# Turning a normalized input by blocks on VectorE instead of on TensorE, in a graph-network layer on one core

## The chip, the cores and the metric

The kernel runs on one core of one Trainium2 chip. The metric is the device time of the whole program in microseconds (us), taken as the median of three runs: 2178.12 us before the change (2177.3 to 2178.31). The profile of the kernel before is of one execution with a span of 2177.0 us.

A core has five engines that run side by side, each through its own list of instructions in a fixed order: TensorE (PE in the profile; its weight loads are listed as PEld), VectorE (DVE), ScalarE (ACT), GpSimd (POOL) and SyncE (SP). Transfers between the on-chip memory (SBUF) and the device memory (DRAM) run on 16 DMA engines; SP, ACT and POOL issue them.

## The reference

For each of 32 graphs ("batches", `b`), with 512 nodes of 256 features:

```python
h = maximum(layernorm(x), 0)            # x: (32, 512, 256), normalized over the features
hc = transpose(h)                       # features first
c  = relu(bn1(conv1d(hc, conv1_w)))     # 1 tap
c  = bn2(conv1d(c, conv2_w, pad 8))     # 17 taps along the nodes
x_conv = transpose(relu(c + hc))
s  = h @ w_se.T + b_se                  # 3 features
A  = exp(-dist(s, s)) * adj             # 512 x 512 for each graph
x_nmp = A @ relu(h @ w_msg.T + b_msg)
out = x + GRU(input=[x_conv, x_nmp], state=h)   # three gates of 256
```

Everything is in float32. What the change touches is the first two lines: each graph's input is normalized with nodes on the partitions (a partition is one of the 128 rows of SBUF), and everything after it wants `h` with the features on the partitions.

## The kernel before

The program lays out its own order of instructions: Python generators ("streams") for the rows, the begins, the graphs, the convolution and the gates take turns, and a clock called `now`, which counts what TensorE's instructions should take, decides which comes next. `yield t` means "go on with other streams until `now` has reached t". The order that results is fixed when the program is built.

The beginning of a graph, from its transfer to the turned and stored copy:

```python
def fetch(b, xs=None):
    XS[b] = front.tile([P, NT, D], F32, name="x_sb", bufs=2) if xs is None else xs
    nc.sync.dma_start(XS[b], x[b].rearrange("(c p) d -> p c d", p=P))

def load(b, xs=None):
    if b not in XS:
        fetch(b, xs)
    NORMS[b] = norm(b)
    NORM_AT[b] = now + 7.0 if b >= G else ARRIVES[b]      # G = 4

def norm(b):
    ...     # VectorE: statistics and rstd; GpSimd: the power of -1/2
    for c in range(NT):                                   # NT = 4
        act.activation(xs[:, c, :], xs[:, c, :], AF.Identity, bias=shift[:, c : c + 1],
                       scale=rstd[:, c : c + 1])
    ...

def norm_t(b, d):
    xn = XS[b]
    if d == 0:
        HT[b] = front.tile([P, ND, N], F32, name="hT", bufs=2)
    ps = bank()                                           # a PSUM bank, "ps_g", 3 of them
    for c in range(NT):
        turn(ps[:, c * P : (c + 1) * P], xn[:, c, d * P : (d + 1) * P])   # TensorE
    act.activation(HT[b][:, d, :], ps, AF.Relu)           # ScalarE
    if d == ND - 1:                                       # ND = 2
        XS.pop(b)
        nc.gpsimd.dma_start(HD[b], HT[b])                 # to DRAM, read again later

def begin(b):
    ...
    yield lambda: b not in NORMS
    yield NORM_AT[b]
    for d in range(ND):
        norm_t(b, d)
        ...         # after the last: begun = b + 1, load(b + 4) or load(b + 2)
        yield now
```

The turned copy in DRAM, `HD[b]`, is read three times: by the first convolution (`load_row`, four graphs at a time), by the messages (`load_graph`) and by the gates (`load_gates`).

Two pieces of the kernel already work by blocks of 32 by 32: from graph 8 on (`TURNED = 8`) the adjacency is loaded in such blocks and turned by VectorE, and so are the output and the residual. A block load, and the last stores:

```python
def blocks(t, dram_b, o, store):
    for g in range(P // 32):
        at = o * P + 32 * g
        a = t[32 * g : 32 * g + 32, :].rearrange("i (k j) -> i k j", j=32)
        d = dram_b[:, :, at : at + 32]
        nc.sync.dma_start(*((d, a) if store else (a, d)))

def store(y, o, s):
    for g in range(P // 32):
        at = slice(32 * g, 32 * g + 32)
        nc.gpsimd.dma_start(OB[b][:, s.start // 32 : s.stop // 32, o * P + 32 * g : ...],
                            y[at, s].rearrange("i (k j) -> i k j", j=32))
```

The graph's stream waits for the first four graphs, because their inputs 2 and 3 lie in its tile `at`:

```python
# graph(b)
    factors_t()
    if b < 1:
        yield lambda: begun >= G
    yield act.free + LAG
    at = front.tile([P, NT, N], F32, name="at", bufs=1)
    kernel_exp(at)                    # four small matmuls, then ScalarE's exp
...
# start of the program
    spare = front.tile([P, NT, N], F32, name="at", bufs=1).rearrange("p c (k d) -> p (c k) d", d=D)
    for b in (2, 3):
        load(b, spare[:, (b - 2) * NT : (b - 1) * NT, :])
```

In the last graph's last gate the products come in two halves, and both halves go to one PSUM tile:

```python
    ps_n = acc.tile([P, N], F32, name="ps_acc")
    ...
    for h in range(2):
        s = slice(h * N // 2, (h + 1) * N // 2)
        for j in range(2 * ND):
            matmul(ps_n[:, s], wih[:, j, cols(o, 2)], x_in[j][:, s], ...)
        mix(s)                        # VectorE reads ps_n[:, s]; then tanh, mixing, store
```

Of the kernel before, what the change touches and what calls it, by code (L numbers as in the profile page):

```python
# [8 lines left out]
F32 = mybir.dt.float32  # L9
AF = mybir.ActivationFunctionType  # L10
# [3 lines left out]
P = 128  # L14
# [17 lines left out]
G = 4  # L32
# [3 lines left out]
TURNED = 8  # L36
# [8 lines left out]
def kernel(  # L45
# [28 lines left out]
    nc = tc.nc  # L74
    B, N, D = x.shape
    NT = N // P
    ND = D // P
# [4 lines left out]
    NZ = 2 * NH  # L82
# [3 lines left out]
    front = ctx.enter_context(tc.tile_pool(name="front", bufs=2))  # L86
    cv = ctx.enter_context(tc.tile_pool(name="cv", bufs=1))
    dram = ctx.enter_context(tc.tile_pool(name="dram", bufs=1, space=bass.MemoryType.DRAM))
    cps = ctx.enter_context(tc.tile_pool(name="cps", bufs=2, space=PSUM))
    bps = ctx.enter_context(tc.tile_pool(name="bps", bufs=1, space=PSUM))  # L90
    acc = ctx.enter_context(tc.tile_pool(name="acc", bufs=2, space=PSUM))
# [6 lines left out]
    now = 5.0  # L98
# [23 lines left out]
    dve, act = Engine(nc.vector, 0.12, 0.00108), Engine(nc.scalar, 0.16, 0.0009)  # L122
# [30 lines left out]
    XS, HT, HB, HR, HG, XN, XR = {}, {}, {}, {}, {}, {}, {}  # L153
    NORMS, NORM_AT = {}, {}
    ARRIVES = (0.0, 7.0, 11.0, 13.0)
    HD = {b: dram.tile([P, ND, N], F32, name=f"hd{b}") for b in range(B)}
    ND_ = {(b, d): dram.tile([P, N], F32, name=f"nd{b}_{d}") for b in range(B) for d in range(ND)}
    begun = told = 0

# [4 lines left out]
    def load(b, xs=None):  # L164
        if b not in XS:
            fetch(b, xs)
        NORMS[b] = norm(b)
        NORM_AT[b] = now + 7.0 if b >= G else ARRIVES[b]

    def load_row(b):  # L170
        HR[b] = front.tile([P, ND, N], F32, name="hT", bufs=2)
        nc.sync.dma_start(HR[b], HD[b])

# [99 lines left out]
    def norm(b):  # L273

        xs = XS[b]
        st = front.tile([P, NT, 6], F32, name="st")
        mv = front.tile([P, NT, 2], F32, name="mv")
        for c in range(NT):
            dve.bn_stats(st[:, c, :], xs[:, c, :])
            dve.bn_aggr(mv[:, c, :], st[:, c, :])  # L280
            if c % 2:
                yield 0.0
        rstd = front.tile([P, NT], F32, name="rstd")
        rsqrt(rstd, mv[:, :, 1])
        yield dve.free + 2.0
        shift = front.tile([P, NT], F32, name="shift")
        dve.scalar_tensor_tensor(
            shift, mv[:, :, 0], -1.0, rstd, op0=ALU.mult, op1=ALU.mult
        )
        yield dve.free + 0.2  # L290
        for c in range(NT):
            act.activation(
                xs[:, c, :], xs[:, c, :], AF.Identity, bias=shift[:, c : c + 1],
                scale=rstd[:, c : c + 1],
            )
            if c % 2:
                yield act.free + LAG
# [291 lines left out]
    xs = all_operands()  # L589
# [174 lines left out]
    XB = x.rearrange("b (k i) d -> b i k d", i=32)  # L764
    OB = out.rearrange("b (k i) d -> b i k d", i=32)

    def blocks(t, dram_b, o, store):
        for g in range(P // 32):
            at = o * P + 32 * g
            a = t[32 * g : 32 * g + 32, :].rearrange("i (k j) -> i k j", j=32)  # L770
            d = dram_b[:, :, at : at + 32]
            nc.sync.dma_start(*((d, a) if store else (a, d)))

    def load_res(b, o):
        if b < B and (b, o) not in XR:
            XR[b, o] = late.tile([P, N], F32, name="res", bufs=3)
            blocks(XR[b, o], XB[b], o, False)

    def begin(b):

        nonlocal begun
        if b == 2:
            yield lambda: told > 0
        yield lambda: b not in NORMS
        yield NORM_AT[b]
        for d in range(ND):
            norm_t(b, d)
            if d == ND - 1:  # L790
                begun = b + 1

                later_b = b + 4 if b < 2 else b + 2 if b >= G else B
                if later_b < B:
                    load(later_b)
            yield now

    def rows(b):
# [8 lines left out]
    def graph(b):  # L807

        nonlocal told
        yield lambda: begun > b  # L810
        if b == 0:
            HG[0] = HT[0]
            yield act.free + LAG
        elif b not in HG:
            load_graph(b)
            yield now + 9.0
        msg = front.tile([P, NT, D], F32, name="msg", bufs=1)
        for c in range(NT):
            messages(b, msg, c)
            yield now  # L820
        told = b + 1
        factors()
        load_graph(b + 1)
        yield dve.free + LAG
        factors_t()
        if b < 1:
            yield lambda: begun >= G
        yield act.free + LAG
        at = front.tile([P, NT, N], F32, name="at", bufs=1)
        kernel_exp(at)  # L830
        yield act.free + 0.3
        for n in range(NT):
            masked(b, at, n)
            if n < NT - 1:
                yield dve.free - 0.2
        settle()
        yield dve.free + LAG
        for d in range(ND):
            gather(b, msg, at, d)
            yield now  # L840

    def gates(b):
# [4 lines left out]
        hT = HB[b]  # L847
# [51 lines left out]
        def store(y, o, s):  # L899
            for g in range(P // 32):  # L900
                at = slice(32 * g, 32 * g + 32)
                nc.gpsimd.dma_start(  # L902
                    OB[b][:, s.start // 32 : s.stop // 32, o * P + 32 * g : o * P + 32 * g + 32],
                    y[at, s].rearrange("i (k j) -> i k j", j=32),
                )
            if s.stop == N:
                del XR[b, o]
                load_res(b + 1, o)

        for o in range(ND):  # L910
            r = z = None

            def reset():
                nonlocal r
                settle()
                r = late.tile([P, N], F32, name="r", bufs=2)
                act.activation(r, ps_r, AF.Sigmoid, bias=brz[:, o : o + 1])

            def reset_hidden():
                dve.scalar_tensor_tensor(  # L920
                    r, ps_h, vec[:, _COL["b_hh"] + 2 * ND + o : _COL["b_hh"] + 2 * ND + o + 1], r,
                    op0=ALU.add, op1=ALU.mult,
                )

            def update():
                nonlocal z
                z = late.tile([P, N], F32, name="z")
                act.activation(z, ps_z, AF.Sigmoid, bias=brz[:, ND + o : ND + o + 1])

            def mix(s=slice(0, N)):  # L930
                dve.tensor_tensor(r[:, s], ps_n[:, s], r[:, s], op=ALU.add)
                later(dve.free + 0.3, lambda r=r, z=z, o=o: mix_next(r, z, o, s))
                if o == ND - 1:
                    load_sums(b + 1, 0)
                    load_sums(b + 1, 1)

            ps_r = acc.tile([P, N], F32, name="ps_acc")
            if o == 0:
                yield lambda: b in evacuated
                yield evacuated[b]  # L940
                yield from residual()
                yield from products(ps_r, o, 0, 0, 1, (0, 2))
                yield act.free + LAG
            else:
                yield from products(ps_r, o, 0, 0, 1, (0, 2))
            yield from products(ps_r, o, 0, 1, 3, (0, 2), reset)
            ps_h = acc.tile([P, N], F32, name="ps_acc")
            yield from products(ps_h, o, 2, 0, 1, (0, 0), reset_hidden)
            ps_z = acc.tile([P, N], F32, name="ps_acc")
            yield from products(ps_z, o, 1, 0, 3, (0, 2), update)  # L950
            if o == 0:
                load_gates(b + 1)
            ps_n = acc.tile([P, N], F32, name="ps_acc")
            if b < B - 1 or o < ND - 1:
                yield from products(ps_n, o, 2, 1, 3, (1, 2), mix)
                continue

            for h in range(2):
                s = slice(h * N // 2, (h + 1) * N // 2)
                for j in range(2 * ND):  # L960
                    matmul(
                        ps_n[:, s], wih[:, j, cols(o, 2)], x_in[j][:, s],
                        start=(j == 0), stop=(j == 2 * ND - 1),
                    )
                mix(s)
                yield now
            settle()
# [96 lines left out]
    )  # L1064
    NORM_AT[0] = act.free + LAG
    load(1)
    spare = front.tile([P, NT, N], F32, name="at", bufs=1).rearrange("p c (k d) -> p (c k) d", d=D)
    for b in (2, 3):
        load(b, spare[:, (b - 2) * NT : (b - 1) * NT, :])
    nc.sync.dma_start(wmsg[:, :, :D], w_msg)  # L1070
    nc.sync.dma_start(wmsg[:, :, D:], w_se)
    nc.sync.dma_start(bmsg[:, :D], b_msg.to_broadcast([P, D]))
# [6 lines left out]
    while streams:  # L1079
# [7 lines left out]
        name = min(able, key=lambda k: clock[k])  # L1087
# [63 lines left out]
```

## Time and profile before

| engine | busy, us | what it does here |
|---|---|---|
| TensorE (PE) | 2113.7 | all products, and the turns of inputs and of the first 8 adjacencies |
| VectorE (DVE) | 1494.1 | transforms of the convolution, mixing of gates, block turns |
| ScalarE (ACT) | 784.4 | normalization, exp, gates, copies out of PSUM |
| GpSimd (POOL) | 282.9 | small powers, and the issue of stores |

A row of the profile's group list names the program line, the engine, the operation, the tile written and the tiles read, the shape and the count, then busy time and mean duration of one, then how long the engine stood idle just before and what released it. A matmul's listed duration includes its way through a pipeline, so the distance between the starts of two matmuls, read from the timeline, tells what one costs TensorE. Names such as L118, L127 and L132 are those of helpers through which nearly all instructions pass, so that the tile names tell the instructions apart. The timeline lists instructions in order of time: start, length, engine, line, operation, tiles, how many were merged, and in brackets the idle time before the first of them.

### The profile page before, as it was taken

The numbers are of one execution on the slowest core, as the hardware profiler recorded it, in microseconds if no ns is written. First come the engines' busy times: TensorE is split into PE (matmuls) and PEld (weight loads), VectorE is DVE, ScalarE is ACT, GpSimd is POOL, SyncE is SP. The second block draws the span as 40 slices with busy tenths as digits, with TensorE's granted clock in tenths as the row PEclk, the third lists the DMA queues.
The fourth block names the chain that finished last, engine by engine and source line by source line (L and its number), as shares of the span: only waits on it lengthen the run. The fifth ranks groups of instructions, "written<-read, shape, count | busy, mean of one in ns | idle before, by whom it ended". The sixth has DMA issues, their size and how long they took to land.

```text
span 2177.0 us, 26672 instructions
## 1 busy us (share of the span) xinstructions
PE 2113.7 (97%) x9392; PEld 1314.7 (60%) x9392; DVE 1494.1 (69%) x2770; ACT 784.4 (36%) x1323; POOL 282.9 (13%) x429
## 2 busy tenths in 40 slices
PE   6999899999999999999999999999999999999997
PEld 3877666566665666656665666656666566665443
DVE  6696886676766767667875777757777677776333
ACT  6445332433233443234424253243522324223211
POOL 2000111111101111101111111101111010011112
PEclk9999999999999999999999999999999999999999
DMA  6346655556574556655665655655565555554231
GB/s 254 143 152 222 204 181 181 159 144 176 153 205 138 146 156 176 189 159 137 180 167 171 185 157 158 178 140 169 158 172 150 150 160 144 151 154 97 61 71 34
DMA packets 432709, 341.94 MB, mean 157 GB/s; under 512 B 351424, under 2 KB 368192, under 8 KB 431936
## 3 DMA queue, kind: packets, MB, share of 16 engines
q1 hardware_dynamic: 408928, 270.23, 45.0%
q0 software_dynamic: 20048, 56.91, 8.4%
q10 hardware_dynamic: 3600, 13.11, 1.5%
q8 instruction: 74, 1.21, 0.2%
q14 instruction: 59, 0.48, 0.1%
HBM read 270.16 MB, written 69.99 MB: 156 GB/s over the span
## 4 chain that ended last, share of the span: by engine, by line
PE 58%; issue 31%; DVE 4%; POOL 3%; ACT 2%; DMA 2%; ACTq 0%; POOLq 0%; SPq 0%; DVEq 0%
PE ps_acc L127 25%; PE ps_g L127 14%; PE ps_c L127 12%; PE ps_b L127 5%; POOL out_dram L902 3%; PE ps_g L132 2%; DMA x_sb<-in_x_dram 1%; PE ps_b L732 1%; DVE x L118 1%; DVE g L118 1%; POOL nd L760 0%; ACT y L118 0%; DVE gg L118 0%; DVE at L118 0%; DVE z L118 0%
## 5 line engine op out<-in xcount | busy, mean ns | idle before, releaser
L127 PE MATMUL ps_acc<-xconv,wih 128*128 128x512 f32 (+1 forms) x772 | 363.5, 593 | 5.8 <-ACT xconv L118 5.2
L127 PE MATMUL ps_acc<-xnb,wih 128*128 128x512 f32 (+1 forms) x772 | 362.5, 592 | 0.0
L127 PE MATMUL ps_acc<-hTb,whh 128*128 128x512 f32 x768 | 355.7, 593 | 0.8 <-ACT r L118 0.8
L127 PE MATMUL ps_c<-xd,w 128*128 128x116 f32 x2800 | 343.0, 276 | 0.0
L127 PEld LDWEIGHTS ps_c<-xd,w 128*128 128x128 f32 x2800 | 328.6, 193 | 3.0 <-issue 2.2
L902 POOL DMA_DIRECT2D out_dram<-res x260 | 169.0, 656 | 1005.0 <-DVE res L118 889.2
L118 DVE TENSOR_TENSOR r<-ps_acc,r 128x512 f32<-128x512 f32 (+1 forms) x65 | 44.4, 684 | 367.3 <-PE ps_acc L127 367.3
L127 PE MATMUL ps_g<-at,msg 128*128 128x512 f32 x512 | 232.0, 602 | 9.6 <-DVE at L118 7.7
L127 PEld LDWEIGHTS ps_acc<-xconv,wih 128*128 128x128 f32 x772 | 141.7, 191 | 160.7 <-issue 149.4
L127 PEld LDWEIGHTS ps_acc<-xnb,wih 128*128 128x128 f32 x772 | 141.2, 189 | 157.9 <-issue 156.3
L127 PEld LDWEIGHTS ps_acc<-hTb,whh 128*128 128x128 f32 x768 | 141.3, 190 | 147.5 <-issue 142.1
L127 PEld LDWEIGHTS ps_b<-x,w 128*128 128x128 f32 x1400 | 182.8, 192 | 68.9 <-issue 53.4
L118 ACT ACTIVATE mid<-ps_b 128x232 f32<-128x232 f32 x175 | 64.0, 366 | 350.4 <-PE ps_b L127 322.3
L127 PE MATMUL ps_b<-x,w 128*128 128x116 f32 x1400 | 184.1, 275 | 5.1 <-ACT at L118 4.7
L127 PEld LDWEIGHTS ps_g<-at,msg 128*128 128x128 f32 x512 | 97.0, 193 | 125.2 <-issue 111.2
L118 DVE SCALAR_TENSOR_TENSOR x<-x,x 128x480 f32<-128x480 f32 (+1 forms) x184 | 144.2, 784 | 3.0
L118 DVE TENSOR_TENSOR x<-x 128x240 f32<-128x240 f32 (+1 forms) x320 | 134.9, 463 | 0.4
L127 PE MATMUL ps_g<-wmsg,hTg 128*128 128x259 f32 x496 | 124.3, 382 | 0.0
L127 PE MATMUL ps_g<-hT,w 128*128 128x512 f32 x256 | 118.2, 605 | 5.2 <-ACT hT L118 4.1
L127 PEld LDWEIGHTS ps_g<-wmsg,hTg 128*128 128x128 f32 x496 | 92.6, 190 | 44.2 <-issue 32.8
L118 ACT ACTIVATE h<-ps_g,bn_shift,bn_scale 128x252 f32<-128x252 f32 (+1 forms) x192 | 81.3, 496 | 102.8 <-PE ps_g L127 102.6
L118 DVE TENSOR_TENSOR xd<-x 128x480 f32<-128x480 f32 x175 | 113.8, 651 | 4.2 <-PE ps_c L127 4.1
(106 smaller groups left out, 2464.4 us busy)
## 6 DMA issues: line engine op xcount, KB each, us to landing
w<-wd SPq DMA_DIRECT2D x150, 768.0 KB, 5.4
m_sb<-in_adj_dram SPq DMA_DIRECT2D x384, 64.0 KB, 2.7
hd<-hT POOLq DMA_DIRECT2D x32, 512.0 KB, 6.5
res<-in_x_dram SPq DMA_DIRECT2D x256, 64.0 KB, 4.7
hTb<-hd SPq DMA_DIRECT2D x32, 512.0 KB, 5.3
xnb<-nd SPq DMA_DIRECT2D x64, 256.0 KB, 2.7
out_dram<-res POOLq DMA_DIRECT2D x252, 64.0 KB, 3.3
hTg<-hd SPq DMA_DIRECT2D x31, 512.0 KB, 3.8
```

What stands on the lines that cost most here:

```text
L118: getattr(self.engine, name)(*tiles, **more)
L127: nc.tensor.matmul(ps, lhsT, rhs, **more)
L132: nc.tensor.transpose(ps, a, ident)
L732: nc.tensor.matmul(pss[c], gr.left[k, :], gr.right[k, :], start=True, stop=True, tile_position=(32 * c, 0),)
L902: nc.gpsimd.dma_start(OB[b][:, s.start // 32 : s.stop // 32, o * P + 32 * g : o * P + 32 * g + 32], y[at, s].rearrange("i (k j) -> i k j", ...
```

## The change

From graph 8 on, the input is no longer turned by TensorE. ScalarE's normalization applies the relu too; the normalized tile is stored as it is to a new DRAM tile `XD_[b]`; it is read back in 32 by 32 blocks to the same SBUF tile, so that each block stands where its transpose belongs; VectorE turns all blocks inside themselves, and the result goes to `HD[b]` as before. It is meant to take the turns off TensorE.

Three smaller parts go with it. Inputs 2 and 3 go to the tile `y` of the convolution, which is not yet in use, so that graph 0 need not wait for them; the statistics of inputs from graph 4 on are held back until `now` is 50. The stores of the last half tiles are issued by SP and ACT in turn instead of by POOL. The last half's products get a PSUM tile of their own.

```diff
+    XD_ = {b: dram.tile([N, D], F32, name=f"xd{b}") for b in range(TURNED, B)}
...
-        NORM_AT[b] = now + 7.0 if b >= G else ARRIVES[b]
+        NORM_AT[b] = max(now + 7.0, 50.0) if b >= G else ARRIVES[b]
...
-                xs[:, c, :], xs[:, c, :], AF.Identity, bias=shift[:, c : c + 1],
+                xs[:, c, :], xs[:, c, :], AF.Identity if b < TURNED else AF.Relu, bias=shift[:, c : c + 1],
...
     def begin(b):
         nonlocal begun
+        if b >= TURNED:
+            yield lambda: b not in NORMS
+            xs = XS.pop(b)
+            nc.gpsimd.dma_start(XD_[b].rearrange("(c p) d -> p c d", p=P), xs)
+            yield now + 4.5
+            xb = xs.rearrange("p c d -> p (c d)").rearrange("p (o n) -> p o n", o=ND)
+            for o in range(ND):
+                blocks(xb[:, o, :], XD_[b].rearrange("(k i) d -> i k d", i=32), o)
+            yield now + 8.0
+            HT[b] = front.tile([P, ND, N], F32, name="hT", bufs=2)
+            for o in range(ND):
+                dve.transpose(HT[b][:, o, :], xb[:, o, :])
+                if o < ND - 1:
+                    yield dve.free
+            nc.gpsimd.dma_start(HD[b], HT[b])
+            begun = b + 1
+            if b + 2 < B:
+                load(b + 2)
+            return
...
         factors_t()
-        if b < 1:
-            yield lambda: begun >= G
         yield act.free + LAG
...
-                nc.gpsimd.dma_start(
+                queue = nc.gpsimd if s.stop - s.start == N else nc.scalar if g % 2 else nc.sync
+                queue.dma_start(
...
             for h in range(2):
                 s = slice(h * N // 2, (h + 1) * N // 2)
+                if h > 0:
+                    ps_n = acc.tile([P, N], F32, name="ps_acc")
...
-    spare = front.tile([P, NT, N], F32, name="at", bufs=1).rearrange("p c (k d) -> p (c k) d", d=D)
+    spare = cv.tile([P, 3, 3, NZ], F32, name="y").rearrange("p e f n -> p (e f n)")
     for b in (2, 3):
-        load(b, spare[:, (b - 2) * NT : (b - 1) * NT, :])
+        at = (b - 2) * NT * D
+        load(b, spare[:, at : at + NT * D].rearrange("p (c d) -> p c d", d=D))
```

(`blocks` also loses its unused way of storing; that changes no instruction.)

More of the change, by code (lines that the diff above doesn't have):

```diff
@@ L765, with blocks @@
     OB = out.rearrange("b (k i) d -> b i k d", i=32)
-    def blocks(t, dram_b, o, store):
+    def blocks(t, rows, o):
         for g in range(P // 32):
             at = o * P + 32 * g
-            a = t[32 * g : 32 * g + 32, :].rearrange("i (k j) -> i k j", j=32)
-            d = dram_b[:, :, at : at + 32]
-            nc.sync.dma_start(*((d, a) if store else (a, d)))
+            nc.sync.dma_start(
+                t[32 * g : 32 * g + 32, :].rearrange("i (k j) -> i k j", j=32),
+                rows[:, :, at : at + 32],
+            )
     def load_res(b, o):
@@ L776, in load_res @@
             XR[b, o] = late.tile([P, N], F32, name="res", bufs=3)
-            blocks(XR[b, o], XB[b], o, False)
+            blocks(XR[b, o], XB[b], o)
     def begin(b):
         nonlocal begun
+        if b >= TURNED:
[17 more added lines that the diff above has]
+            return
         if b == 2:
@@ L791, in begin @@
                 begun = b + 1
-                later_b = b + 4 if b < 2 else b + 2 if b >= G else B
-                if later_b < B:
-                    load(later_b)
+                if b < 2 or b >= G:
+                    load(b + (G if b < 2 else 2))
             yield now
```

## The prediction, made before the changed kernel was run

> **What bounds the kernel now.** I read the page first: shares of busy time and the forty slices. Then I cut the span into stretches, looked at who waited for whom, and opened the timeline at the start, at one graph in the middle and at the end. The page's first part (engine, busy us, share, instructions) and its line on packets:
>
> ```profile
> PE 2113.7 (97%) x9392; PEld 1314.7 (60%) x9392; DVE 1494.1 (69%) x2770; ACT 784.4 (36%) x1323; POOL 282.9 (13%) x429
> ...
> DMA packets 432709, 341.94 MB, mean 157 GB/s; under 512 B 351424, under 2 KB 368192, under 8 KB 431936
> ```
>
> TensorE is idle for only 2177.0 - 2113.7 = 63.3 us. The table of stretches (length, then busy us of PE, PEld, DVE, ACT and POOL, the granted clock, DMA share and GB/s) says where:
>
> ```profile
> 44.60:53.10 8.50, 1.94 (x3) 0.49 (x2) 8.40 (x18) 6.50 (x12) 0.59 (x1) 0.68 0.67 264
> 53.10:63.00 9.90, 9.90 (x68) 9.85 (x68) 3.13 (x8) 3.18 (x6) 0.00 (x0) 0.75 0.20 82
> ...
> 400.00:800.00 400.00, 396.96 (x1752) 245.05 (x1749) 277.94 (x515) 147.45 (x244) 53.07 (x76) 1.00 0.57 162
> 800.00:1200.00 400.00, 398.85 (x1748) 244.67 (x1746) 278.32 (x528) 149.43 (x258) 51.28 (x73) 1.00 0.60 163
> ```
>
> In the middle PE lacks 1 to 3 us in 400; DVE has 30% free and the DMA engines 40%. So in the middle only work taken off PE shortens the program, and only new waits of PE lengthen it. About 22 us of the idle time lie before 53 us and about 12 us after 2160 us.
>
> **What one turn costs.** The page gives the turns of inputs 280 ns each, but that is with their way through the pipeline. The timeline around one graph (PE) gives the distance:
>
> ```profile
> 1023.82 7.04 PE L127 MATMUL ps_g<-at,msg 128*128 128x512 f32 x16
> 1030.69 1.04 PE L132 MATMUL ps_g<-ident,x_sb 128*128 128x128 f32 x8
> 1031.57 1.88 PE L127 MATMUL ps_acc<-xconv,wih 128*128 128x512 f32 x4
> ```
>
> Eight turns occupy 1031.57 - 1030.69 = 0.88 us, 0.11 us each, with no idle time before them.
>
> **What the Trainium skill says.** "VectorE: DVE Perf Modes", section "The three transpose paths": VectorE turns 32 by 32 blocks, each by itself, and only TensorE turns 128 by 128 in one go. That is why a way through DRAM is needed to put the blocks in place. The trace already has such turns: `STREAM_TRANSPOSE right<-m_sb 128x512`, 96 of them, mean 705 ns. "DMA: Bandwidth & Descriptors", section "Specifications": at least 512 B per piece are needed for line rate. The block loads have pieces of 32 floats, 128 B, and the trace agrees: an adjacency tile of 64 KB in such pieces lands 2.7 us after its issue, one of 256 KB in whole rows after 2.8 us. Same page, section "Two DMAs through the same engine are not ordered": a transfer that reads what another wrote has to wait for that one's completion semaphore, on whatever queue it is. So the store's whole time lies ahead of the block loads; no such pair with so short a distance is in the trace before. "TensorE: Matmul & The Clock Gate", section "Part 1: The HAM clock gate (the "warmup" mystery)": an idle window of about 3.4 us halves the clock until TensorE has been busy again. The start agrees:
>
> ```profile
> 43.00 1.60 PE L732 MATMUL ps_g<-right,left 5*128 5x512 f32 x4
> 51.16 2.07 PE L732 MATMUL ps_g<-right,left 5*128 5x512 f32 x2 [6.56 <-ACT hT L118]
> 53.16 9.68 PE L127 MATMUL ps_c<-x,w 128*128 128x116 f32 x64
> 62.67 0.60 PE L132 MATMUL ps_g<-ident,x_sb 128*128 128x128 f32 x4
> 63.11 3.73 PE L127 MATMUL ps_c<-x,w 128*128 128x116 f32 x32
> ```
>
> The first 64 products of the convolution take 9.5 us start to start; at the pace of the next 32 (3.56 us) they would take 7.1 us. The clock in that stretch is 0.75.
>
> **Part 1, the turns.** Graphs 8 to 31 are 24; 24 x 8 = 192 turns x 0.11 us = 21.1 us leave PE, all in stretches where PE is the bound: -21.1 us. ScalarE loses 48 copies out of PSUM at 0.54 us (1.08 us for a pair in the timeline), 26 us, and DVE gains 48 turns x 0.705 = 34 us, from 69% to about 71%. Neither bounds the middle, so both count zero by themselves. The DMA engines get 24 stores of 512 KB and 24 x 8 block loads, 24 x 4096 = 98304 more packets of 128 B. The queue that carries nearly all packets moves 408928 of them in 45.0% of 16 engines' span, 38 ns each; at that mean, an estimate, the new ones take 3.7 ms over 16 engines, 233 us, or 15% of the 1550 us in which they lie. The share there goes from about 0.58 to about 0.74.
>
> **Part 2, new waits.** Here the program's own clock matters: loads are placed 4.5 us after the store, VectorE's turns 8 us after the loads. The trace has the durations: `hd<-hT`, the same 512 KB from POOL, lands after 7.0 us in the median in the middle (up to 8.7). So SP stands some 2.7 us at the first block load, which costs nothing unless another load behind it is urgent; the convolution's weights are asked for two products ahead, some 20 us (200 products in the span). Eight block loads in a row: in the timeline eight adjacency loads of the same size issue in 5.22 us and land 3.1 us after issue, together 8.3 us. From the store, 0.5 us for its issue, 7.0 for its landing and 8.3 for the loads make 15.8 us; the turns are placed at 12.5 us, with about 1 us more until the stream's turn comes. The first VectorE turn needs only four of the loads, ready at about 11.8 us; the second comes at about 14.3 us and would wait some 1.5 us, more when the DMA engines are full. That is 24 x 1.5 = 36 us of waiting on VectorE. It has 30% to spare and its results are mostly used several us later: operands are made three products ahead, PSUM tiles of the convolution and the gates are doubled. PE meets it only when a tight consumer (the masked kernel, the factors, the residual) lies just behind. I put a seventh of it through: +5 us.
>
> **Part 3, the start.** The 6.56 us gap comes from a PSUM bank: graph 4's turned input sat in it until ScalarE, busy with the first convolution weights, copied it at 50.5 us. With graph 4's statistics held back to 50 us and graph 0's exp no longer behind inputs 2 and 3, both causes go. DVE also loses two sets of statistics (2.3 us each) ahead of its first operands, and a wait of 5.16 us for input 4 at 25 us, ahead of the weights' preparation. The exp, masking and gathering of graph 0 (some 10 us of PE) can fill the holes of 1.9 to 2.4 us between the rows. The first product should start at about 46 instead of 53.2 us; of the 22 us idle about 13 remain, the first 9.2 (input and statistics) in any case, and the cold 2.4 us mostly go too. Against that, weights and operands get less lead, and DVE is 90% busy between 100 and 200 us, so part is given back: -8 us.
>
> **Part 4, the end.** The last stores:
>
> ```profile
> 2163.51 1.13 PE L127 MATMUL ps_acc<-xconv,wih 128*128 128x256 f32 x4 [0.52 <-DVE r L118]
> ...
> 2169.59 4.61 POOL L902 DMA_DIRECT2D out_dram<-res x8 [12.00 <-DVE res L118]
> 2169.67 0.42 DVE L118 TENSOR_TENSOR res<-o_sb,res 128x256 f32<-128x256 f32 x1
> ```
>
> POOL needs 0.58 us for each of eight issues, until 2174.2; the results were there at 2170.1. Two queues with four issues each at 0.48 us (SP's block loads: 1.93 us for four), two of them before the last result, are done at about 2171.3: -2.9 us. The second half's products no longer wait for VectorE to read the first half: another -0.9 us at most, as everything behind is a chain of VectorE and ScalarE. Together -3.5 us.
>
> **Sum.** 2178.1 - 21.1 - 8 - 3.5 + 5 = 2150.5, say 2151 us, 1.2% faster.
>
> **Rivals.** (a) VectorE becomes the wait: the blocks land late under the fuller DMA load (landings of residual blocks spread from 1.9 to 8.1 us), each of the 24 graphs stalls VectorE by 4 to 6 us, and half of that reaches PE: +50 us, time about 2195. For it speaks that the 8 us leave nothing over my 8.3; against it that TensorE now waits for VectorE only a dozen us in all between 130 and 2100 us, with VectorE 70% busy. (b) The fuller DMA queues delay what was just in time, the rows of `hT` placed 8 us behind their load (5.7 us to land now): with 2 us for half of 24 loads +24 us, about 2175, the gain eaten. (c) The start gives nothing, since convolution weights come no faster: about 2158. (d) Everything is hidden and the start fills all its holes: 21 + 12 + 4 gives 2141. A gain of 2% needs 43.6 us, more than the turns and all three smaller parts at their best.
>
> **Range and chances.** The turns are sure to about 1 us; the start is -3 to -12, the end -2.5 to -4.5, the new waits 0 to +25, with a tail. That makes 2138 to 2172 us for 8 in 10. Over 2% faster (under 2134.6) would need gains that I can't name: 0.07. Over 2% slower (above 2221.7) needs rival (a) in full and more: 0.04. Within 2%: 0.89.
>
> **What would show it.** In the profile after: turns of `x_sb` on PE down to 48, PE busy time down by about 21 us plus some cold clock; 48 `hT<-x_sb` turns on DVE of about 0.7 us, with idle time before them "<-DMA" of about 1 to 2 us a graph; the first `ps_c` product near 46 us; the last issues done by about 2.9 us sooner behind the last result. I am wrong if PE's idle time between 200 and 1700 us grows by more than 15 us, or if the first product starts no earlier.

## The result: 2155.2 us, 1.0% faster, with one jam in it

The changed kernel takes 2155.22 us (2153.63 to 2158.26, four runs) where the kernel before takes 2177.71 us (2175.01 to 2178.31, four runs). The ratio is 0.9901, 95% interval 0.9884 to 0.9918. The profile's spans are 2177.0 us before and 2156.5 us after.

The page after, its first part and its line on packets:

```profile
PE 2095.1 (97%) x9200; PEld 1299.9 (60%) x9200; DVE 1522.5 (71%) x2818; ACT 762.0 (35%) x1277; POOL 295.3 (14%) x445
...
DMA packets 539462, 367.12 MB, mean 170 GB/s; under 512 B 455232, under 2 KB 472000, under 8 KB 538688
```

TensorE has 192 instructions and 18.6 us of busy time less. VectorE has the 48 turns and 28 us more, the packets under 512 B are 103808 more (98304 of them are the new blocks), and TensorE is as full as before. Its idle time is 2156.5 - 2095.1 = 61.4 us, against 63.3. So nearly the whole gain of 20.5 us is busy time, though the start and the end were changed to take idle time away. The stretches tell why. Columns: length, then busy us of PE, PEld, DVE, ACT and POOL, the granted clock, the DMA share and GB/s. Before:

```profile
200.00:260.00 60.00, 52.32 (x304) 37.97 (x304) 40.23 (x75) 29.85 (x52) 4.88 (x9) 0.94 0.72 234
...
400.00:1700.00 1300.00, 1292.86 (x5672) 797.97 (x5669) 915.11 (x1700) 471.87 (x793) 166.12 (x242) 1.00 0.59 164
```

After:

```profile
200.00:260.00 60.00, 41.07 (x219) 28.83 (x218) 36.61 (x68) 25.61 (x44) 5.11 (x10) 0.86 0.81 247
...
400.00:1700.00 1300.00, 1294.19 (x5591) 792.88 (x5588) 943.61 (x1747) 459.88 (x769) 181.68 (x263) 1.00 0.66 180
```

TensorE's idle time by stretch, worked out from such rows (length less PE busy):

| stretch, us | before | after | difference |
|---|---|---|---|
| 0 to 200 | 30.0 | 21.9 | -8.1 |
| 200 to 260 | 7.7 | 18.9 | +11.2 |
| 260 to 400 | 0.9 | 0.8 | -0.1 |
| 400 to 1700 | 7.1 | 5.8 | -1.3 |
| 1700 to 2100 | 2.9 | 4.2 | +1.3 |
| 2100 to the end | 14.6 | 9.8 | -4.8 |

The start gave its 8 us, the end its part, the long middle nothing and took nothing; and between 200 and 260 us 11 us were lost again. That loss is one wait, the jam of the heading. The longest waits of TensorE after 130 us in the changed kernel (waiting tile, what it waited for: us in total, times, longest):

```profile
PE ps_g L132 <- DMA m_sb<-in_adj_dram: 17.3, 1, 17.3
PE ps_b L127 <- ACT at L118: 4.7, 5, 1.6
```

In the timeline of TensorE it stands ahead of the fourth adjacency tile of graph 3, which TensorE still turns (only graphs from 8 on are turned by blocks):

```profile
213.67 0.66 PE L132 MATMUL ps_g<-ident,m_sb 128*128 128x128 f32 x4 [0.49 <-ACT h L118]
231.61 1.09 PE L132 MATMUL ps_g<-ident,m_sb 128*128 128x128 f32 x4 [17.29 <-DMA m_sb<-in_adj_dram]
232.49 3.15 PE L127 MATMUL ps_acc<-hTb,whh 128*128 128x512 f32 x4
235.48 3.60 PE L127 MATMUL ps_g<-at,msg 128*128 128x512 f32 x8
```

SP's list of issues (SPq; the second figure is the time that the issues took) says where that tile's load was:

```profile
206.41 0.37 SPq L692 DMA_DIRECT2D whh<-in_w_hh_dram  x1
206.83 0.42 SPq L693 DMA_DIRECT2D wih<-in_w_ih_dram  x1
207.36 0.49 SPq L470 DMA_DIRECT2D w<-wd  x1
207.90 14.94 SPq L771 DMA_DIRECT2D res<-in_x_dram  x8
...
224.47 1.00 SPq L262 DMA_DIRECT2D m_sb<-in_adj_dram  x2
```

Behind the gates' weights (whh and wih, 2.3 MB) come the first eight residual block loads (`res`). SP takes 14.94 us to issue them, one alone 7.58 us, with the DMA engines at a share of 1.0. Only then does the adjacency load go out, and it needs 7.0 us to land. The kernel before has the same loads, but there one adjacency load stands ahead of the residual:

```profile
218.14 0.33 SPq L261 DMA_DIRECT2D m_sb<-in_adj_dram  x1
...
219.72 8.14 SPq L772 DMA_DIRECT2D res<-in_x_dram  x8
```

TensorE waited 0.69 us for that adjacency tile there, and 5.84 us for VectorE's mask (`at`):

```profile
227.28 6.05 PE L127 MATMUL ps_g<-at,msg 128*128 128x512 f32 x8 [5.84 <-DVE at L118]
```

### The profile page after: what moved, and what is told of

The parts are those of the page before. It is cut to its first block, busy times and chain, and to the rows that moved or that the text cites. A ratio compares the mean times of both kernels' runs of the same rounds, so it can differ in the third digit from the quotient of the medians.

```text
span 2156.5 us, 26543 instructions
## 1 busy us (share of the span) xinstructions
PE 2095.1 (97%) x9200; PEld 1299.9 (60%) x9200; DVE 1522.5 (71%) x2818; ACT 762.0 (35%) x1277; POOL 295.3 (14%) x445
## 4 chain that ended last, share of the span: by engine, by line
PE 94%; DVE 2%; ACT 2%; SPq 1%; DMA 1%; issue 0%; ACTq 0%; POOL 0%; DVEq 0%; POOLq 0%
PE ps_acc L127 46%; PE ps_g L127 20%; PE ps_c L127 18%; PE ps_b L127 7%; PE ps_g L132 2%; PE ps_b L733 1%; SPq L771 1%; ACT at L118 0%; DVE x L118 0%; DMA m_sb<-in_adj_dram 0%; ACT xconv L118 0%; DVE xconv L118 0%; ACT w L118 0%; DVE g L118 0%; PE ps_g L733 0%
## 5 line engine op out<-in xcount | busy, mean ns | idle before, releaser
L922 POOL DMA_DIRECT2D out_dram<-res x252 | 164.2, 657 | 977.1 <-DVE res L118 878.6
L127 PE MATMUL ps_g<-at,msg 128*128 128x512 f32 x512 | 226.8, 593 | 1.1 <-DVE at L118 1.1
L118 ACT ACTIVATE z<-ps_acc,brz 128x512 f32<-128x512 f32 x64 | 44.0, 687 | 208.7 <-PE ps_acc L127 208.4
```

Of the source, the lines that this page charges most:

```text
L118: getattr(self.engine, name)(*tiles, **more)
L127: nc.tensor.matmul(ps, lhsT, rhs, **more)
L922: queue.dma_start(OB[b][:, s.start // 32 : s.stop // 32, o * P + 32 * g : o * P + 32 * g + 32], y[at, s].rearrange("i (k j) -> i k j", j=32),)
```

## Experiments

Times are given as ratios to the kernel before, run on the same chip at the same time, with their 95% intervals; 0.001 is 2.2 us. One kernel's runs differ with the granted clock: of the kernel before, 31 runs timed with experiments 1, 3, 5 and the first of 4 take 2174.1 us on average at a mean clock of 0.994 and 2178.5 us at 0.992, so a few us between two profiles can be the clock of those two runs.

### 1. The jam: residual loads later

```diff
 # all_gates
-        for o in range(ND):
-            load_res(0, o)
 # gates(b), o == 0
                 yield from residual()
+                for k in range(ND if b == 0 else 0):
+                    load_res(0, k)
```

> The changed kernel with one thing moved: the first eight residual block loads are issued after graph 0's convolution output has been added up, no longer ahead of the adjacency loads on SP's queue. The order on TensorE stays the same. Theory (one blocked queue): the single wait of 17.3 us at 214 us, TensorE for m_sb, falls to under 7 us, and the time by 9 to 13 us, to about 2144 us. Rival (the DMA engines are full there, share 1.0, whatever order the loads have): the wait stays above 13 us and the time at 2152 to 2157 us.

Measured: 2149.1 us, ratio 0.9876 (0.9861 to 0.9891); the changed kernel had 0.9901 (0.9884 to 0.9918), so the intervals still overlap at their edges. The edit moves loads only and leaves TensorE's order alone. The waits of TensorE in this run:

```profile
PE ps_g L132 <- DMA m_sb<-in_adj_dram: 8.5, 1, 8.5
```

The wait went from 17.3 to 8.5 us, so half of it was the blocked queue, and the span from 2156.5 to 2148.8 us. It did not fall under 7 us as expected, nor did the time fall by 9 us: the medians differ by 6.1 us, the ratios by 5.4. The rival, that order doesn't matter, falls too. SP's list shows the rest: the adjacency load now goes out at 214.24 us, as soon as its buffer is free, and takes 9.95 us, with the DMA engines still full (a share of 0.95 to 1.11 from 213 to 225 us).

### 2. The jam: the gates' second weights later too

```diff
 # late_pools
-        nc.sync.dma_start(wih, w_ih)
 # gates(b), o == 0, on top of experiment 1
+                if b == 0:
+                    nc.sync.dma_start(wih, w_ih)
```

> The changed kernel with the late first residual loads, and with the gates' weights wih (1.5 MB) loaded behind graph 0's last adjacency tile too; TensorE first reads them some 20 us later. Theory (what is left of the wait for m_sb, 8.5 us with the late residual loads alone, is time in which the DMA engines are full of loads that nobody needs yet): 1.5 MB at some 410 GB/s are 3.7 us, so the wait falls to 3 to 6 us and the time by 3 to 6 us below that with late residual loads alone. Rival (the wait is set by when the adjacency buffer comes free and by latency): the wait stays at 7 us or more and the time the same within 1.5 us.

Measured: 2148.41 us, ratio 0.9872 (0.9856 to 0.9888). The wait:

```profile
PE ps_g L132 <- DMA m_sb<-in_adj_dram: 4.9, 1, 4.9
```

8.5 to 4.9 us is 3.6 us, as 1.5 MB of earlier traffic should make it, and the profiled run is the shortest of all, 2143.2 us. The medians don't confirm the step: 2148.41 against 2149.1 us is no difference that these runs resolve. So the wait's cause is shown, as two moves of loads took it from 17.3 to 4.9 us; its worth in time is some 6 us for both moves together (0.9872 against 0.9901), with intervals that overlap at their edges. Both versions are clearly faster than the kernel before.

When this wait is long can be read from the SP lists and waits of the other experiments. With the start alone (experiment 4) the residual's loads also stand ahead of the adjacency's, but convolution products are placed before the turn that needs it, and TensorE does not wait for the adjacency at all. With the block turns alone (experiment 3) the adjacency load goes out ahead of the residual, and the wait is 3.0 us. With both, but without the hold (the last run of experiment 4), it is 13.1 us. So the long wait comes with the turns and the new start together, not with either alone.

### 3. The block turns alone

> The kernel before with the block turns alone: start and last stores as before. Theory: the turns are worth their 192 x 0.11 us in full, as VectorE's waits for blocks don't reach TensorE: 2156 to 2160 us, unless the start's order makes the same jam of loads, then up to 2170. Rival (block waits on VectorE eat part of it): 2165 to 2175 us with TensorE's idle time between 400 and 1700 us grown by 5 us or more.

The edit is the changed kernel with the start, the hold of the statistics to 50 and the end put back. Measured: 2165.12 us, ratio 0.9952 (0.9933 to 0.9971), 10.7 us less than the median before, 2175.79 us. TensorE's stretches in this run:

```profile
200.00:260.00 60.00, 47.65 (x252) 34.66 (x251) 35.95 (x70) 23.34 (x44) 5.07 (x9) 0.86 0.78 256
...
400.00:1700.00 1300.00, 1294.15 (x5597) 790.76 (x5596) 947.15 (x1758) 464.33 (x776) 183.76 (x266) 1.00 0.66 181
```

Busy time fell by 20.4 us (2113.7 to 2093.4), and from 400 to 1700 us TensorE is idle for 5.9 us against 7.1 before: there the turns are worth all they cost. From 200 to 260 us it is idle for 12.4 us against 7.7. The time lies where I had put the turns with a jam of loads, up to 2170 us, though the jam in this profile is a small one; it is the low end of the rival's time too, but the rival's sign, idle time grown in the middle, isn't there. Of the 20.4 us, 5.2 come back as idle time in the profile, 4.7 of them between 200 and 260 us, which leaves the 15.2 us by which the spans differ. That the medians differ by only 10.7 us comes from which runs were profiled: the profiled run before (2179.1 us) lies 3.3 us above the median of the runs timed here, the profiled run of this experiment 1.5 us below its own.

### 4. The start, in pieces

> The kernel before with the changes of the start alone: inputs 2 and 3 in the tile y, no wait of graph 0, statistics from graph 4 on held back to 50. Theory: about 8 us of TensorE's idle time before 200 us go, so 2170 us; if the jam at the first residual loads comes with it, 2178 to 2182 us and a TensorE wait for m_sb of over 10 us near 215 us. Rival (the start gives nothing): 2176 to 2179 us with the first ps_c product later than 52 us.

> The kernel before with only the statistics of inputs from graph 4 on held back to 50. Theory (most of the start's gain is the bank held by graph 4's turned input, the 6.56 us gap): 4 to 7 us less than before, 2171 to 2174 us. Rival (the gain comes from graph 0's exp and gathers filling holes): less than 3 us.

> The kernel before with inputs 2 and 3 in the tile y and graph 0 not waiting for them, and nothing else. Theory (TensorE's holes at the start are filled by graph 0, and this alone does it): TensorE's idle time in the first 50 us falls from 20 us to under 14, and the time to 2170 to 2175 us. Rival (without the hold of the statistics the order is no better, as the hold alone made it worse): 2178 us or more.

> The changed kernel without the hold of the statistics to 50; inputs 2 and 3 still in the tile y. Theory (the hold was there for TensorE's 6.56 us gap, and graph 0's early exp makes that gap small anyway): 0 to 4 us slower than the changed kernel. Rival (the hold is what gains at the start): over 5 us slower, with TensorE waiting for ACT hT near 45 us again.

| run | edit | ratio (interval) | TensorE idle 0 to 200 us | PE busy in all |
|---|---|---|---|---|
| before | | 1 | 30.0 | 2113.7 |
| start alone | tile `y`, no wait, hold | 0.9981 (0.9972 to 0.9989) | 22.1 | 2119.8 |
| hold alone | statistics held to 50 | 1.0042 (1.0029 to 1.0055) | 27.3 | 2123.2 |
| tile alone | tile `y`, no wait | 0.9961 (0.9949 to 0.9974) | 21.0 | 2111.0 |
| changed kernel without the hold | turns, tile `y`, end | 0.9899 (0.9884 to 0.9915) | 20.4 | 2093.5 |

The tile alone does it: 8 us, though TensorE's idle time in the first 50 us fell from 20.0 to 15.2 us only, not under 14. The 6.56 us gap is gone without the hold; the longest wait in its place is 2.62 us. The hold alone makes the kernel slower by 9 us, where I expected it to carry most of the gain; in the changed kernel it makes no difference that can be measured (0.9899 without, 0.9901 with). What the hold does can be read from TensorE's timeline with the tile alone,

```profile
49.15 5.22 PE L127 MATMUL ps_g<-at,msg 128*128 128x512 f32 x8 [2.62 <-DVE at L118]
54.21 7.30 PE L127 MATMUL ps_c<-x,w 128*128 128x116 f32 x64
61.34 0.60 PE L132 MATMUL ps_g<-ident,x_sb 128*128 128x128 f32 x4
```

and with the hold, in the changed kernel:

```profile
49.20 10.87 PE L127 MATMUL ps_c<-x,w 128*128 128x116 f32 x96
59.91 3.61 PE L127 MATMUL ps_g<-at,msg 128*128 128x512 f32 x8
66.68 3.35 PE L127 MATMUL ps_c<-x,w 128*128 128x116 f32 x16 [3.17 <-ACT w L118]
69.82 2.15 PE L132 MATMUL ps_g<-ident,x_sb 128*128 128x128 f32 x12
```

With the hold the convolution starts 5 us sooner, uses up its weights and waits 3.17 us for ScalarE to make the next; the 16 products after that take 3.14 us start to start where the pace is 1.78 us. In the run with the start alone, which has the same order there, PE's busy time is 8.8 us above that with the tile alone, while its idle time in the first 200 us is about the same. The work is the same, and the mean granted clock is 0.990 against 0.993. Two stretches are slower in it: 60 to 70 us, with 0.83 against 1.00, and 220 to 230 us, with 0.66 against 0.85; the slow ones around 105 and 145 us (0.83 and 0.66) are in both runs. The profiled run of the start alone is the slowest of its twelve, so 8.8 us is at the high end; the ratios differ by 4.4 us.

### 5. The end alone

> The kernel before with the changes of the end alone: last half stores on SP and ACT, the second half's products in a PSUM tile of their own. The order on TensorE and VectorE stays. Theory: 3 to 4 us less, 2174 us; from TensorE's last matmul to the end 8.5 us in place of 11.5, and no wait of about 0.9 us before the second half. Rival (the end is bound by the landing of the stores, not their issue): less than 1.5 us.

Measured: ratio 0.9987 (0.998 to 0.9994), 1.3 to 4.4 us less. The interval reaches below the rival's 1.5 us, so the time doesn't decide; the trace does better. In the changed kernel, whose end is the same:

```profile
2146.09 1.03 PE L127 MATMUL ps_acc<-xconv,wih 128*128 128x256 f32 x4
2146.29 0.42 DVE L118 TENSOR_TENSOR r<-ps_acc,r 128x256 f32<-128x256 f32 x1 [6.06 <-PE ps_acc L127]
...
2148.02 0.42 DVE L118 TENSOR_TENSOR r<-ps_acc,r 128x256 f32<-128x256 f32 x1 [1.30 <-PE ps_acc L127]
...
2151.79 1.82 SPq L922 DMA_DIRECT2D out_dram<-res  x4
2151.79 1.92 ACTq L922 DMA_DIRECT2D out_dram<-res  x4
```

The second half's first matmul starts ahead of VectorE's read of the first. The read of the last products before:

```profile
2165.54 0.42 DVE L118 TENSOR_TENSOR r<-ps_acc,r 128x256 f32<-128x256 f32 x1 [2.09 <-PE ps_acc L127]
```

From that read to the end of the program it is 2156.5 - 2148.02 = 8.5 us, against 2177.0 - 2165.54 = 11.5 before: 3.0 us. From the first half's first matmul (2144.37, before 2161.10) to that read it is 3.65 us against 4.44: 0.8 us. The run of the end alone has 8.1 and 3.66 us.

### 6. How much of a VectorE wait reaches TensorE

```diff
-            yield now + 8.0
+            yield now + 2.0
             HT[b] = front.tile([P, ND, N], F32, name="hT", bufs=2)
```

> The changed kernel with VectorE's turns placed 2 us behind the block loads in place of 8, so that VectorE has to stand and wait for nearly every graph. It measures how much of a VectorE wait reaches TensorE. Theory (VectorE's free 28% and the results made ahead take it up): VectorE idle before hT<-x_sb grows from 21 us to 80 to 150 us, and the time grows by less than 15 us. Rival (a VectorE wait goes through to TensorE by half or more): the time grows by 40 us or more.

Measured: 2161.58 us, ratio 0.9927 (0.9908 to 0.9946). VectorE's idle time ahead of its turns grew from 21.1 us in 4 waits to 51.1 us in 14, less than I had expected. Of these, from 400 to 1700 us, 21.1 grew to 40.7 us, and TensorE's idle time there from 5.8 to 7.5 us: 1.7 of 19.6 us, about a tenth, went through. In time it is 5.7 us more than the changed kernel by the ratios, with intervals that overlap. The rival's 40 us are excluded.

### 7. More graphs turned by blocks

> The changed kernel with the late first residual loads, and with block turns of inputs and adjacency from graph 6 on in place of 8: 2 x (8 + 16) = 48 turns less on TensorE at 0.11 us, 5.3 us, for 2 x (2 + 4) = 12 VectorE turns and 4 x 2 VectorE products that are there already. Theory: about 5 us less than with 8 and late loads, if VectorE (86% busy between 100 and 200 us) can take it. Rival: VectorE's load in the first 250 us gives it back, no difference or up to 5 us slower.

> The same from graph 4 on: 96 turns less than with 8, 10.6 us. Theory: 8 to 11 us less than with 8 and late loads. Rival: as VectorE still prepares the convolution's weights until 200 us, TensorE waits for it there, and the time is that with 8 or longer.

Measured: from graph 6 on 0.9991 (0.9983 to 1.0), from graph 4 on 0.9916 (0.9897 to 0.9935), against 0.9876 with 8 and late residual loads. Both are slower, the one from graph 6 on by 25 us. The theory fell, but the rival's place is at best half right. With 6, TensorE is idle for 23.7 us between 400 and 1700 us against 5.8, and before 200 us for 23.1 us against 21.5. Its waits from 260 to 2100 us are led by others:

```profile
PE ps_acc L127 <- ACT r L118: 12.0, 6, 4.7
PE ps_b L127 <- ACT at L118: 8.8, 12, 0.8
PE ps_c L127 <- DVE z L118: 5.7, 3, 2.6
```

With 4, TensorE's idle time before 200 us is 27.2 us, 5.7 more, where the rival put it, though on weights that come from ScalarE (8.1 us against 3.5); another 12.6 us more lie from 260 to 2100 us. An edit that touches a few early graphs shifts the order of everything after them, and these orders are worse ones. That the shifted order is the cause is not shown by itself; which shift it would be was not followed.

### 8. Without the start, and without the jam

> The version with late residual loads and late wih, with the changes of the start undone: it says what the start is worth where no jam of loads hides it. Theory: TensorE's idle time before 200 us grows by 8 us and its cold stretches shrink by 4 to 6, so 2 to 5 us slower than the same with the start. Rival (the start is worth its full 8 us): 7 to 10 us slower.

Measured: 2161.7 us, ratio 0.9938 (0.9918 to 0.9957), 14 us above experiment 2. Neither theory has that much. In the profile TensorE's idle time before 200 us is 8.8 us more (30.9 against 22.1), which is the start. Another 5.5 us lie between 200 and 400 us, 2.7 of them a wait for the late wih, which this order needs sooner. So the run doesn't give the start's worth cleanly; 8.8 us of idle time is what can be said.

## Why the prediction was right, and where it wasn't

2151 us was predicted, 2155.2 measured, inside 2138 to 2172. By its steps:

**What bounds the kernel, and the turns: right.** TensorE's bound held in the middle, 192 turns went, and experiment 3 shows 20.4 us less busy time with no idle time in their place from 400 to 1700 us; 21.1 us was the step. A part of it can still be lost elsewhere: the same experiment has 4.7 us more idle time between 200 and 260 us.

**New waits: +5 us came out as +11 us, by another way.** The step was that VectorE would wait 1.5 us for its blocks in each of 24 graphs, 36 us, and a seventh reach TensorE. The group of turns and what VectorE waited for ahead of them in the changed kernel (durations in ns; then us, times):

```profile
L118 DVE STREAM_TRANSPOSE hT<-x_sb x48: 665/703/712, 192.8 to 1609.6; 128x512 f32<-128x512 f32 x48
...
  DMA x_sb<-xd: 21.1, 4
```

Four waits, not 24. The term that was mis-sized is the chain from store to blocks, 15.8 us in the sum:

```profile
xd<-x_sb POOLq DMA_DIRECT2D x24, 512.0 KB, 4.0
x_sb<-xd SPq DMA_DIRECT2D x192, 64.0 KB, 2.7
```

The store lands after 4.0 us in the median, not the 7.0 of `hd<-hT`, and by the prediction's own sum that alone puts the blocks (12.8 us) ahead of the second turn (14.3 us) in most graphs. The DMA engines' share between 400 and 1700 us rose from 0.59 to 0.66, half of the 0.15 reckoned for the new packets. Experiment 6 puts the share that goes through at about a tenth; the seventh was near. What did come is a single wait of TensorE on the adjacency, at 214 us. That the term's +5 us stands beside +11 us, inside its range of 0 to 25, is luck: in the middle, where the waits were reckoned, TensorE's idle time fell by 1.3 us. The prediction had its mechanism in half a sentence, that SP's standing "costs nothing unless another load behind it is urgent", and rival (b), that fuller queues delay what was just in time; but it placed it at the new block loads and the rows of `hT`, not where the residual's first block loads meet 2.3 MB of weights. TensorE's idle time from 200 to 1700 us grew by 9.8 us, under the 15 us that the prediction set as its sign of being wrong.

**The start: the size right, the cause half wrong.** -8 us of idle time were predicted and -8.1 measured (before 53 us there were 21.1 us to take, not 22). The step that failed is "With graph 4's statistics held back to 50 us and graph 0's exp no longer behind inputs 2 and 3, both causes go": the hold is worth nothing or costs time (experiment 4), the tile, with graph 0 no longer waiting, is all of it, and with the hold alone TensorE waits 4.71 us for ScalarE in the gap's place. So the size came out by the half of the step that had graph 0's work fill the holes. Wrong too is the sign I gave for it, the first convolution product near 46 us. It came at 49.2 us, and with the tile alone at 54.2, later than before, with a better time: what fills TensorE's holes is graph 0's work, not an earlier convolution. "The cold 2.4 us mostly go" held where it was said, as the first 96 products now take 10.71 us, the pace of 1.78 us for 16; but the new order has cold stretches of its own. Busy time fell by 18.6 us with 21.1 us of turns gone, so the same work took 2.5 us longer; the mean granted clock went from 0.992 to 0.989. How much of this is the order stays open, as profiles of the same work in experiments 1, 2 and 4 have 2092.3 to 2096.5 us of busy time.

**The end: right.** 2.9 + 0.9 us were the terms, 3.0 + 0.8 the trace.

In the spans the sum is -21.1 + 2.5 of busy time and -8.1 + 11.2 - 4.9 (the other stretches together) of idle time, -20.5 us with rounding, where -27.6 was predicted: the long wait makes its stretch 6 us more than its term, and the clock is 2.5 us that had none. With most of the jam gone the kernel runs at 2148 to 2149 us.

## What to carry to other kernels

When an engine is full, work taken off it counts in full only where it stays full; read the gain by stretch, and look in each stretch for one long wait before adding up many short ones. A load that is wanted at once shares its issuing queue and the DMA engines with everything placed ahead of it, so where big weights arrive in the middle of a program, put what nobody needs yet behind what is needed next. Starting a pipeline sooner gained nothing here (experiment 4), as its suppliers couldn't follow: the wait only moved, and the clock fell behind it.

## What the runs showed of the hardware that was not expected

A transfer of 64 KB can hold its issuing queue for 7.58 us, where the median is 0.49 us, when the DMA engines are at a share of 1.0. Two stores of 512 KB from the same queue differ in the median: 4.0 us to land for `xd` (3.4 to 9.9), 5.9 us for `hd<-hT` (3.0 to 9.0) in the same run; why was not tried. After a wait of 17.29 us four matmuls took 2.99 us start to start where the pace is 1.72 us, with a granted clock of 0.58 in that stretch and 0.50 in the 13.6 us before it, so a wait costs more than its length. This agrees with what the prediction cited from the Trainium skill, "TensorE: Matmul & The Clock Gate", Part 1, on idle windows. The traces of experiment 4 add that shorter waits than the 3.4 us cited there also had slow products behind them: after 3.17 us, 3.14 us in place of 1.78, and after 2.62 us, 5.06 us for eight products in place of the 3.43 us at the pace of the prediction's timeline (6.87 us for 16).
